# More room for weight combinations, later loads and single-pass degrees at the beginning of a graph and attention kernel

## The chip, the core and the metric

The kernel runs on one core of a Trainium2 chip. The metric is the device time of one execution in microseconds (us). Five engines work side by side, each in the order of its own instructions: TensorE (PE in the profile; its weight loads are PEld), VectorE (DVE), ScalarE (ACT), GpSimd (POOL) and SyncE (SP), which here only issues transfers. They wait for each other by semaphores. [...]

## The reference

32 batches of 512 nodes with 512 features, one adjacency matrix. Each batch passes a graph layer and an attention layer, both with a residual and a LayerNorm:

```python
a = adj.astype(x.dtype); deg = a.sum(axis=1)
mi = einsum('bkd,od->bko', x, Wi); mj = einsum('bkd,od->bko', x, Wj)
x = layernorm(x + deg[None, :, None] * (mi + b) + einsum('ij,bjo->bio', a, mj))
q, k, v = heads(x @ Wq.T + bq), heads(x @ Wk.T + bk), heads(x @ Wv.T + bv)   # 8 heads of 64
scores = where(adj == 0, -inf, q @ k.T / 8)
x = layernorm(x + (softmax(scores) @ v) @ Wo.T + bo)
```

## The kernel before

The kernel multiplies weights by a scheme of seven products of 256 x 256 blocks in place of eight ("pieces" 1 to 7). It needs sums and differences of each weight's quarters. They are made once, at the beginning, stored to DRAM, and later loaded again and again through a ring of seven buffers:

```python
RING = 7
def combine(name, eng, part):
    w = W[name]
    a11, a12, a21, a22 = [w[j][:, :, Q * i:Q * i + Q] for i in range(2) for j in range(2)]
    t = [work([P, 2, N], "e", 4) for _ in range(2 - part)]      # "e": four buffers in all
    t = [u[:, c].rearrange("p (c i) -> p c i", c=2) for u in t for c in range(2)]
    if part == 0:
        s1, s2, s4 = t[:3]
        eng.tensor_tensor(s1, a21, a22, op=OP.add)              # L252
        eng.tensor_tensor(s2, s1, a11, op=OP.subtract)          # L253
        eng.tensor_tensor(s4, a12, s2, op=OP.subtract)          # L254
        ...
    else:
        s3, n22 = t
        eng.tensor_tensor(s3, a11, a21, op=OP.subtract)         # L260
        eng.tensor_scalar(n22, a22, -1.0, 1.0, ...)             # L261
        ...
    for i, u in made:
        WS[name, i] = dram.tile(...)
        nc.sync.dma_start(WS[name, i], u)                       # L265
```

A buffer of a name is given out in turn; whoever takes one again waits until its last readers, here the stores, are done. All loads and stores of this part go through SyncE's queue, in order. The loads at the start, in that order:

```python
load adj, x[0], wi, wj, wv, wq, wk            # 1 MB each
load_x(1)
for q in range(4):
    load_xa(1, q)                             # L113: x[1] in 32 x 32 blocks, pieces of 128 B
wo = load_wo()                                # L166: eight transfers
...                                           # later: b0, bo, bq, bk on GpSimd's queue, bv on SyncE's (L221)
```

`xa` holds x in blocks, so that VectorE can turn it with a transpose of 32 x 32 blocks (L339, `l0_turn`), which GpSimd then multiplies with the degrees. There is one buffer of the name `xa`. The adjacency matrix is turned by TensorE; ScalarE copies it to `adjT` (fp32), VectorE to `adjR` (float32r). The degrees come out of a product with ones:

```python
for jc in range(NC):
    nc.tensor.matmul(pd, ones, adjT[:, jc, :], ...)             # L193, fp32
```

The first batch's graph layer runs with plain products (`plain`, L604), interleaved with the combinations:

```python
def first():
    # half(name, i) is combine(name, engine, i); wi, wj on GpSimd, the others on VectorE
    return [g[0], ..., g[1], g[2], half("wv", 0), g[3], base 0, base 1, half("wv", 1),
            y[0], scaled 0, half("wq", 0), half("wi", 0), y[1], scaled 1, half("wq", 1), half("wi", 1), fold 0,
            y[2], half("wk", 0), half("wj", 0), scaled 2, n[0], y[3], half("wk", 1), half("wj", 1), n[1], fold 1, scaled 3]
# g: gather with adj (L325); y: plain product, residual, LayerNorm statistics (L604, L606, L289, L291)
# scaled: LayerNorm applied by ScalarE (L296); n: turn by TensorE (L353)
```

Then the beginning runs phase c of batch 0 (q, k and v by pieces, L427; the first product of each is copied by ScalarE to p, L434; VectorE adds the others, L456, L465, L472) and phase a of batch 1 (gather, turns, four more pieces of k):

```python
def phase_a(n):
    for i in range(DC):
        res += g[i:i + 1] + k[i:i + 1] + [z(l0_turn, n, i)]
        ...
        if n == 1 and i in (1, 3):
            res += [z(combine, "wo", nc.vector, i // 2)]

PERIODS = [first() + phase_c(0) + phase_a(1)]
```

After it the first scoring period begins: scores (L481), exponential (L485), mask (L486), values (L503), with the pieces of the next batches' graph layers and projections between them. Phase c of later batches also loads the next x:

```python
if i in (6, 7) and 0 < n < B - 1:
    res += [z(load_xa, n + 1, 2 * (i == 7) + (f is v[i]))]
```

Of the kernel before, what the change touches and what calls it, by code (L numbers as in the profile page):

```python
# [10 lines left out]
FR = mybir.dt.float32r  # L11
# [6 lines left out]
P = 128  # L18
# [7 lines left out]
def gnn_attention_kernel(  # L26
# [36 lines left out]
    nc = tc.nc  # L63
    B, N, D = x.shape
    NC = N // P
    DC = D // P
# [13 lines left out]
    def work(shape, name, bufs, dtype=FT):  # L80
        return pools.work.tile(shape, dtype, name=name, bufs=bufs)

    def big():
        return work([P, 4, N], "big", 6)

    def mm_tile(bank):
        return psum.tile([P, 512], FT, name="mm" + bank, bufs=1)
# [7 lines left out]
    def turn_tile():  # L95


        return sc_tile()[:, 0, :]
# [9 lines left out]
    def load_xa(b, q):  # L108

        if q == 0:  # L110
            XA[b] = work([P, DC, N], "xa", 1)
        src = x[b].rearrange("(t p) (c q f) -> q p c t f", p=32, q=4, f=32)
        nc.sync.dma_start(XA[b][32 * q:32 * q + 32].rearrange("p c (t f) -> p c t f", f=32), src[q])  # L113

    def load_x(b):
        XT[b] = work([P, NC, D], "xh", 3)
        nc.sync.dma_start(XT[b], rows(x[b]))
# [12 lines left out]
    def load_w(t, src, eng):  # L130
        eng.dma_start(t, rows(src))
        return t
# [15 lines left out]
    ones = const.tile([P, P], FT, name="ones")  # L148
# [5 lines left out]
    for name, src in (("wv", wvT), ("wq", wqT)):  # L154
        t = load_w(work([P, NC, D], "v", 2), src, nc.sync)
        W[name] = [t[:, 0:2, :], t[:, 2:4, :]]
    load_halves("wk", wkT, "q", nc.sync)
    load_x(1)
    for q in range(4):
        load_xa(1, q)  # L160

    def load_wo():
        t = work([P, NC, D], "xh", 3)
        for h in range(4):
            for g in range(2):
                nc.sync.dma_start(t[32 * h:32 * h + 32, 2 * g:2 * g + 2], woT.rearrange("(g h r d) o -> g h d r o", g=2, h=4, r=2)[g, h])  # L166
        return t

    wo = load_wo()
# [6 lines left out]
    def turned(adj_f, t, also=None):  # L176
        for jc in range(NC):
            pt = turn_tile()
            for ic in range(NC):
                nc.tensor.transpose(pt[:, ic * P:(ic + 1) * P], adj_f[:, ic, jc * P:(jc + 1) * P], ident)  # L180
            nc.scalar.copy(t[:, jc, :], pt)
            if also is not None:
                nc.vector.tensor_copy(also[:, jc, :], pt)
        return t
# [3 lines left out]
    adjR = const.tile([P, NC, N], FR, name="adjR")  # L188
    adjT = turned(adj_f, big(), adjR)
    deg_r = const.tile([P, N], FT, name="deg_r")  # L190
    pd = mm_tile("a")
    for jc in range(NC):
        nc.tensor.matmul(pd, ones, adjT[:, jc, :], start=(jc == 0), stop=(jc == NC - 1))  # L193
    deg_c = const.tile([P, NC], FT, name="deg_c")

    SPLIT = {}
# [44 lines left out]
    def ring_tile():  # L241
        return work([P, 2, Q], "ring", RING)

    def combine(name, eng, part):

        w = W[name]
        a11, a12, a21, a22 = [w[j][:, :, Q * i:Q * i + Q] for i in range(2) for j in range(2)]
        t = [work([P, 2, N], "e", 4) for _ in range(2 - part)]
        t = [u[:, c].rearrange("p (c i) -> p c i", c=2) for u in t for c in range(2)]
        if part == 0:  # L250
            s1, s2, s4 = t[:3]
# [3 lines that stand above are left out]
            made = ((6, s2), (5, s1), (3, s4))  # L255
            if name == "wo":
                made += ((1, a11), (2, a12))
        else:
            s3, n22 = t
            eng.tensor_tensor(s3, a11, a21, op=OP.subtract)  # L260
            eng.tensor_scalar(n22, a22, -1.0, 1.0, op0=OP.mult, op1=OP.mult)  # L261
            made = ((7, s3), (4, n22))
        for i, u in made:
            WS[name, i] = dram.tile([P, 2, Q], FT, name=f"{name}_{i}")
            nc.sync.dma_start(WS[name, i], u)  # L265
# [115 lines left out]
    def quarter(src, j, n):  # L381
        return src[:, 2 * j:2 * j + 2, Q * n:Q * n + Q]
# [168 lines left out]
    def z(f, *a):  # L551
        return (0.0, f, *a)
# [9 lines left out]
    def banks(n):  # L562

        return ("a", "b") if n % 2 == 0 else ("b", "a")

    def phase_a(n):

        A, K = banks(n)
        if n == B:
            return [pc("k", n - 1, i, bank) for i, bank in ((6, K), (5, A), (7, K), (3, A), (4, K))]  # L570
        xq, aq = lambda j, m: quarter(XD[n], j, m), lambda j, m: quarter(AX_T[n], j, m)
        g = [(GA, l0_gather, n, dc, A) for dc in range(DC)]
        k = [pc("k", n - 1, i, K) for i in LATE]
        res = []
        for i in range(DC):
            res += g[i:i + 1] + k[i:i + 1] + [z(l0_turn, n, i)]
            if i in (1, 2):
                res += [z(base, n, i - 1)]
            if n == 1 and i in (1, 3):
                res += [z(combine, "wo", nc.vector, i // 2)]  # L580
            if i == 1:
                res += [z(combos, TX, n, xq, (1,)), z(combos, TA, n, aq, (1,))]
        return res + [z(combos, TX, n, xq, (2,)), z(combos, TA, n, aq, (2,)),
                      z(combos, TX, n, xq, (3, 4)), z(combos, TA, n, aq, (3, 4)),
                      pc("l0", n, 1, A), k[4]]
# [36 lines left out]
    def phase_b(n):  # L622

        m = n - 2
        if m < 0:
            res = []
            side = [z(add_bo, 0, i) for i in range(2)]
            A, K = banks(n)
            for i, bank in ((2, A), (6, K), (5, A), (7, K), (4, K), (3, A)):
                res.append(pc("l0", n, i, bank))  # L630
                if i == 4:
                    res += [z(stats, n, 0)]
                res += side[:1]
                side = side[1:]
            return res + [z(apply, n, 0), z(stats, n, 1), (TR, l0_norm, n, 0), (TR, l0_norm, n, 1)]
        A = banks(n)[0]
        l0 = {i: pc("l0", n, i, A) for i in ORDER}
        return [l0[2], *project(m, 1), l0[6], *project(m, 2), l0[7], z(add_bo, n - 1, 0), *project(m, 6), l0[4], z(stats, n, 0),
                *project(m, 7), z(apply, n, 0), z(h_store, n, 0), l0[5], z(h_load, n, 0), z(add_bo, n - 1, 1), *project(m, 4),
                l0[3], z(stats, n, 1), z(h_turn, n, 0), *project(m, 5)]  # L640

    def phase_c(n):

        m = n - 2
        norm = [(TR, l0_norm, n, ic) for ic in range(NC)]
        h = lambda j, i: quarter(HT[n], j, i)
        A, K = banks(n)
        v, q, k = [{i: pc(kind, n, i, bank) for i in ORDER} for kind, bank in (("v", A), ("q", K), ("k", A))]
        if m < 0:
            res = [v[1]] + ([z(apply, n, 1)] if n else []) + [q[1], v[2], norm[2], norm[3], z(combos, TH, n, h, (1, 2)), k[1],  # L650
                                                             z(combos, TH, n, h, (3, 4)), q[2], k[2]]
        else:
            res = [z(apply, n, 1), z(h_store, n, 1), v[1], *project(m, 3), z(h_load, n, 1), z(stats, m, 0), v[2], z(stats, m, 1),
                   q[1], k[1], z(apply, m, 0), z(h_turn, n, 1), q[2], z(apply, m, 1), z(store, m),
                   z(combos, TH, n, h, (1, 2)), z(combos, TH, n, h, (3, 4)), k[2]]
        side = []
        if n == 0:

            side = [z(graph_forms, 2), None, z(graph_forms, 0), None, z(graph_forms, 1)]
        for i in LATE:  # L660
            for f in q[i], v[i]:
                res += [f] + [g for g in side[:1] if g]
                side = side[1:]
                if i in (6, 7) and 0 < n < B - 1:
                    res += [z(load_xa, n + 1, 2 * (i == 7) + (f is v[i]))]
            if i == 3 and 0 < n < B - 1:
                res += [z(load_x, n + 1)]
            if i == 7 and n + 1 < B:
                res += [z(ahead, n + 1)]
        return res  # L670
# [145 lines left out]
    with tc.If(flag > 0), tc.tile_pool(name="general", bufs=1) as pools.work:  # L816
        wi, wj, wv, wq, wk, wo = [load_w(work([P, DC, D], f"w{i}", 1), src, nc.sync)
                                  for i, src in enumerate((wiT, wjT, wvT, wqT, wkT, woT))]
# [2 lines left out]
        adj_f = big()  # L821
        nc.vector.tensor_copy(adj_f, adj_i)
        adj_t = turned(adj_f, work([P, NC, N], "adj_t", 1))

        bias_m = work([P, NC, N], "bias_m", 1)
        nc.vector.tensor_scalar(bias_m, adj_i, 0.0, -BIG, op0=OP.is_equal, op1=OP.mult)
# [16 lines left out]
        with tc.For_i(0, B, 1) as b:  # L843
# [22 lines left out]
            for hp in range(HP):  # L866
# [6 lines left out]
                for qb in range(NC):  # L873
# [23 lines left out]
                    for kc in range(NC):  # L897
                        for s in range(2):
                            c0 = hp * P + s * HD
                            nc.tensor.matmul(pm[s * HD:(s + 1) * HD, :P], V[g][:, kc, c0:c0 + HD], pT[:, s, kc, :],  # L900
                                             start=(kc == 0), stop=(kc == NC - 1))
# [48 lines left out]
```

## Time and profile before

| what | value |
|---|---|
| time, median of 3 | 3706.04 us (3705.42 to 3707.18) |
| span of the profiled execution | 3701.0 us |
| mean granted TensorE clock | 0.998 |
| moved by DMA | 530.02 MB, mean 143 GB/s |

An entry such as `PE mma L427` names the engine, the tile written and the line of the kernel. `x8` is a count of instructions. A bracket such as `[3.07 <-ACT p L434]` is the idle time of the engine just ahead, and what ended it. SPq is SyncE's queue; the time beside it is the time to issue, not to land. A table by stage gives for each stretch the busy time of PE, PEld, DVE, ACT and POOL with their counts, then TensorE's granted clock, the share of the DMA engines and GB/s.

### The profile page before, as it was taken

What the parts mean: (1) busy time and instruction counts of PE and PEld (TensorE: products, weight loads), DVE (VectorE), ACT (ScalarE), POOL (GpSimd) and SP (SyncE); (2) the same over time, 40 slices, a digit from 0 to 9 for tenths busy, and PEclk for the clock granted to TensorE, in tenths of its full rate; (3) what the DMA queues carried; (4) which work ended last, traced back from release to release, by engine and by line L of the source; (5) the groups of instructions that cost most, each with busy time, mean ns of one, the idle gap of its engine ahead of it and who ended that gap; (6) DMA issues with size and microseconds to landing.
All of it is one profiled execution on the core that took longest, in us unless ns stands there. A gap on an engine that the chain in (4) does not pass through costs nothing.

```text
span 3701.0 us, 49651 instructions
## 1 busy us (share of the span) xinstructions
PE 3664.3 (99%) x18474; PEld 2511.5 (68%) x18474; DVE 2390.7 (65%) x3134; ACT 1028.4 (28%) x1482; POOL 1938.8 (52%) x1985
## 2 busy tenths in 40 slices
PE   8999999999999999999999999999999999999998
PEld 5666666666676767676767666666666676767663
DVE  4566766666666666666666666666666666666665
ACT  2222232322322222222232222232222322222322
POOL 3465545555455564455554555545555545555443
PEclk9999999999999999999999999999999999999999
DMA  7444555455564445554555544555544556445541
GB/s 250 127 126 134 151 151 162 122 143 137 154 159 142 128 135 151 157 155 125 137 143 157 159 135 134 137 149 160 148 132 132 147 151 164 124 136 140 151 137 47
DMA packets 797173, 530.02 MB, mean 143 GB/s; under 512 B 530432, under 2 KB 611840, under 8 KB 796928
## 3 DMA queue, kind: packets, MB, share of 16 engines
q1 hardware_dynamic: 780384, 494.78, 49.7%
q10 hardware_dynamic: 16320, 31.46, 2.3%
q8 instruction: 151, 2.47, 0.3%
q14 instruction: 94, 0.77, 0.1%
q0 software_dynamic: 224, 0.53, 0.0%
HBM read 453.25 MB, written 73.40 MB: 142 GB/s over the span
## 4 chain that ended last, share of the span: by engine, by line
PE 96%; DVE 1%; SPq 1%; POOL 1%; DMA 0%; issue 0%; ACT 0%; POOLq 0%; DVEq 0%; ACTq 0%
PE mma L427 31%; PE mmb L427 31%; PE sc L481 13%; PE ov L503 13%; PE mmb L325 3%; PE mma L325 3%; PE sc L513 2%; SPq L113 0%; DVE rl L522 0%; DVE e L486 0%; DMA wv<-e 0%; SPq L144 0%; DVE st L289 0%; PE sc L727 0%; POOL es L492 0%
## 5 line engine op out<-in xcount | busy, mean ns | idle before, releaser
L485 ACT ACTIVATE sc<-sc 128x1024 f32<-128x1024 f32 x512 | 493.2, 1007 | 1552.5 <-PE sc L481 1546.2
L486 DVE TENSOR_TENSOR e<-sc,edge 128x1024 f32<-128x1024 f32 x512 | 602.2, 1217 | 206.3 <-ACT sc L485 174.3
L427 PE MATMUL mmb<-ring,big 128*128 128x256 f32 x3144 | 731.7, 381 | 0.0
L427 PE MATMUL mma<-ring,big 128*128 128x256 f32 x3112 | 725.3, 382 | 4.2 <-ACT p L434 3.1
L427 PEld LDWEIGHTS mmb<-ring,big 128*128 128x128 f32 x3144 | 592.0, 190 | 131.5 <-issue 26.8
L427 PEld LDWEIGHTS mma<-ring,big 128*128 128x128 f32 x3112 | 586.3, 190 | 135.2 <-issue 26.0
L396 POOL TENSOR_TENSOR big<-big 128x512 f32<-128x512 f32 x376 | 492.7, 1338 | 32.4 <-ACT big L354 11.7
L481 PE MATMUL sc<-q,k 64*128 64x512 f32 x2048 | 509.1, 615 | 0.0
L503 PE MATMUL ov<-e,v 128*32 128x512 f32 x4096 | 492.5, 598 | 4.9 <-DVE oT L538 4.9
L492 POOL TENSOR_TENSOR es<-e 128x1024 f32<-128x1024 f32 x128 | 300.0, 2355 | 351.7 <-DVE e L486 351.7
L427 PE MATMUL mma<-big,ring 128*128 128x256 f32 x1808 | 430.3, 381 | 3.2 <-DVE k L465 3.2
L427 PE MATMUL mmb<-big,ring 128*128 128x256 f32 x1776 | 422.8, 381 | 1.0 <-DVE v L456 1.0
L291 POOL TENSOR_SCALAR mv<-mv 128x1 f32<-128x1 f32 x256 | 49.6, 194 | 671.6 <-DVE mv L290 659.1
L427 PEld LDWEIGHTS mma<-big,ring 128*128 128x128 f32 x1808 | 340.5, 190 | 76.5 <-issue 26.0
L427 PEld LDWEIGHTS mmb<-big,ring 128*128 128x128 f32 x1776 | 334.4, 190 | 73.4 <-issue 26.0
L503 PEld LDWEIGHTS ov<-e,v 128*32 128x32 f32 x4096 | 107.0, 109 | 352.2 <-issue 320.8
L204 POOL TENSOR_TENSOR xlo<-xh,xhi 128x512 fp32r<-128x512 f32 x128 | 163.6, 1289 | 337.6 <-ACT xhi L203 337.6
L481 PEld LDWEIGHTS sc<-q,k 64*128 64x128 f32 x2048 | 176.1, 186 | 207.3 <-issue 205.1
L340 POOL TENSOR_TENSOR big<-big,deg_r 128x512 f32<-128x512 f32 x124 | 173.6, 1400 | 266.3 <-DVE big L339 266.3
L494 DVE TENSOR_TENSOR es<-es,e 128x1024 f32<-128x1024 f32 x250 | 304.2, 1217 | 0.0
L445 DVE TENSOR_TENSOR xh<-xh,mma 128x512 f32<-128x512 f32 x186 | 126.6, 681 | 267.0 <-PE mma L427 267.0
L445 DVE TENSOR_TENSOR xh<-xh,mmb 128x512 f32<-128x512 f32 x186 | 126.7, 681 | 263.0 <-PE mmb L427 263.0
(155 smaller groups left out, 3656.2 us busy)
## 6 DMA issues: line engine op xcount, KB each, us to landing
ring<-wo SPq DMA_DIRECT2D x217, 256.0 KB, 2.8
ring<-wq SPq DMA_DIRECT2D x160, 256.0 KB, 3.9
ring<-wv SPq DMA_DIRECT2D x160, 256.0 KB, 3.4
ring<-wk SPq DMA_DIRECT2D x160, 256.0 KB, 3.2
ring<-wi SPq DMA_DIRECT2D x155, 256.0 KB, 2.7
ring<-wj SPq DMA_DIRECT2D x155, 256.0 KB, 2.7
xh<-in_x_dram SPq DMA_DIRECT2D x32, 1024.0 KB, 5.4
xa<-in_x_dram SPq DMA_DIRECT2D x124, 256.0 KB, 4.0
```

The lines of the kernel that those rows point to most:

```text
L204: nc.gpsimd.tensor_sub(lo, xs, hi.bitcast(FT))
L325: nc.tensor.matmul(pm, parts[w][:, jc, :], adjR[:, jc, :], start=(w == 0 and jc == 0), stop=(w == 1 and jc == NC - 1))
L340: nc.gpsimd.tensor_tensor(XD[b][:, dc, :], XD[b][:, dc, :], deg_r, op=OP.mult)
L396: nc.gpsimd.tensor_tensor(dst, p, q, op=OP.subtract)
L427: nc.tensor.matmul(pm[:, c * Q:(c + 1) * Q], lhs, rhs, start=first, stop=(kc == 1 and n == len(terms) - 1), skip_group_check=True)
L445: nc.vector.tensor_tensor(d, d, pm, op=OP.add)
L481: nc.tensor.matmul(ps[:, s, :], KT[b, hp // 2][r, hp % 2, kc * P:(kc + 1) * P], QT[b, hp // 2][r, hp % 2, :], start=True, stop=True)
L485: nc.scalar.activation(ps, ps, AF.Exp, scale=QSCALE)
L486: nc.vector.tensor_tensor(e, ps, edge[:, kc:kc + 1, :].to_broadcast([P, 2, N]), op=OP.mult)
L492: nc.gpsimd.tensor_add(ES[i], E[i, 0], E[i, 1])
L494: nc.vector.tensor_add(ES[i], ES[i], E[i, kc])
L503: nc.tensor.matmul(PV[g][r][32 * h:32 * h + 32, :], V[b][:, kc, c0:c0 + 32], E[h // 2, kc][:, h % 2, :], start=(kc == 0), stop=(kc == NC - 1))
```

## The change

It does four things. The combinations of wq and of wi's second part get buffers of names that are not yet in use at that time (`xa`, `es`), so that the four `e` buffers are needed less often. wo's combinations move out of phase a of batch 1 into the first scoring period, into `oT` buffers. The second batch's x in blocks is loaded in phase c of batch 0, as for later batches, and no longer ahead of wo. The degrees are computed with float32r operands from `adjR` and a copy of the ones. A branch for unusual inputs, which does not run here, computes its degrees in fp32 as before.

```diff
     load_x(1)
-    for q in range(4):
-        load_xa(1, q)
@@
     deg_r = const.tile([P, N], FT, name="deg_r")
+    onesR = work([P, P], "rl", 1, FR)
+    nc.scalar.copy(onesR, ones)
     pd = mm_tile("a")
     for jc in range(NC):
-        nc.tensor.matmul(pd, ones, adjT[:, jc, :], start=(jc == 0), stop=(jc == NC - 1))
+        nc.tensor.matmul(pd, onesR, adjR[:, jc, :], start=(jc == 0), stop=(jc == NC - 1))
@@
+    def room(name, part):
+
+        if name == "wq" and part == 0:
+            t = work([P, DC, N], "xa", 1)
+            return [t[:, 0:2, :], t[:, 2:4, :]]
+        if (name, part) in (("wq", 1), ("wi", 1)):
+            return [work([P, 2, N], "es", 2)]
+        return [work([P, 2, N], "oT" if name == "wo" else "e", 3 if name == "wo" else 4) for _ in range(2 - part)]
+
     def combine(name, eng, part):
@@
-        t = [work([P, 2, N], "e", 4) for _ in range(2 - part)]
+        t = room(name, part)
@@
-            s3, n22 = t
+            s3, n22 = t[:2]
@@ phase_a
-            if n == 1 and i in (1, 3):
-                res += [z(combine, "wo", nc.vector, i // 2)]
@@ phase_b, the layer-0 pieces of batch 1, in the first scoring period
                 if i == 4:
                     res += [z(stats, n, 0)]
+                if i in (2, 6):
+                    res += [z(combine, "wo", nc.vector, int(i == 6))]
@@ phase_c
-                if i in (6, 7) and 0 < n < B - 1:
+                if i in (6, 7) and n < B - 1:
                     res += [z(load_xa, n + 1, 2 * (i == 7) + (f is v[i]))]
@@ the branch for unusual inputs
+        pd = mm_tile("a")
+        for jc in range(NC):
+            nc.tensor.matmul(pd, ones, adj_t[:, jc, :], start=(jc == 0), stop=(jc == NC - 1))
+        nc.scalar.copy(deg_r, pd)
```

## The prediction

> **What bounds the kernel now.** I read the page first: the span, the busy shares and the 40 slices.
>
> ```profile
> span 3701.0 us, 49651 instructions
> PE 3664.3 (99%) x18474; PEld 2511.5 (68%) x18474; DVE 2390.7 (65%) x3134; ACT 1028.4 (28%) x1482; POOL 1938.8 (52%) x1985
> ...
> PE   8999999999999999999999999999999999999998
> ```
>
> TensorE is busy in 3664.3 of 3701.0 us, so 36.7 us of idle time are left in the whole execution. Only the first and the last slice are below 9. The change touches only the beginning, so the next view is the table of busy time by stage.
>
> ```profile
> 8.00:16.00 8.00, 7.45 (x26) 4.60 (x25) 2.76 (x4) 3.82 (x7) 3.26 (x4) 1.00 1.04 391
> 52.00:72.00 20.00, 15.38 (x56) 10.32 (x55) 9.59 (x18) 6.11 (x10) 13.07 (x18) 0.91 0.79 279
> 104.00:112.00 8.00, 4.83 (x23) 3.80 (x22) 7.93 (x8) 0.58 (x1) 5.35 (x4) 1.00 0.36 130
> 160.00:300.00 140.00, 140.00 (x717) 96.45 (x718) 90.89 (x118) 40.65 (x61) 73.52 (x69) 1.00 0.52 141
> ```
>
> The first number after the stage's length is TensorE's busy time. From 160 us on it is full: 140.00 of 140.00. Idle time sits in 52 to 72 us (4.62 us, and the granted clock falls to 0.91) and in 104 to 112 us (3.17 us). Who causes it is told by the waits of TensorE between 20 and 160 us:
>
> ```profile
> PE mma L427 <- DVE k L465: 3.2, 1, 3.2
> PE mma L427 <- ACT p L434: 3.1, 1, 3.1
> PE sc L353 <- ACT xh L296: 1.5, 1, 1.5
> ```
>
> These are three single waits, 7.8 us together; nothing else there exceeds 0.8 us. The timeline gives the cause of each. Columns are start, duration, engine and line; the bracket is the idle time before it.
>
> ```profile
> 11.29 4.23 PE L193 MATMUL mma<-big,ones 128*128 128x512 f32 x8
> 15.08 16.27 SPq L113 DMA_DIRECT2D xa<-in_x_dram  x4
> 31.39 4.63 SPq L166 DMA_DIRECT2D xh<-in_woT_dram  x8
> 39.90 1.33 SPq L265 DMA_DIRECT2D wv<-e  x3
> 43.04 0.69 DVE L254 TENSOR_TENSOR e<-v,e 128x512 f32<-128x512 f32 x1 [7.01 <-DMA wv<-e]
> 51.56 1.26 POOL L254 TENSOR_TENSOR e<-k,e 128x512 f32<-128x512 f32 x1 [5.28 <-DMA wv<-e]
> 52.80 0.69 DVE L260 TENSOR_TENSOR e<-v 128x512 f32<-128x512 f32 x1 [7.53 <-DMA wq<-e]
> 66.27 2.94 PE L427 MATMUL mma<-ring,big 128*128 128x256 f32 x8 [3.07 <-ACT p L434]
> 104.88 1.78 DVE L252 TENSOR_TENSOR e<-xh 128x512 f32<-128x512 f32 x1
> 106.69 1.63 DVE L253 TENSOR_TENSOR e<-e,xh 128x512 f32<-128x512 f32 x1
> 109.70 1.99 PE L427 MATMUL mma<-big,ring 128*128 128x256 f32 x8 [3.17 <-DVE k L465]
> ```
>
> The chain behind the first two waits: the SyncE queue spends 16.27 us issuing the blocked loads of the second batch's x. Behind them, in order, stand wo's load and the bias, so wv's first combinations are stored only at 39.90 us. Four e buffers hold all combinations, so VectorE waits 7.01 and 7.53 us and GpSimd 5.28 us for stores. LayerNorm statistics and scales stand behind these combinations in the same engines' order. The scale of row block 3 (L296) ends at 65.7 us, and only then does ScalarE copy the product p1 for which the matmuls at 66.27 us wait. The third wait is different: wo's first combinations (L252 to L254) occupy VectorE from 104.88 to 109.05 us, and k's addition L465 stands behind them.
>
> [...] the degrees' four fp32 matmuls are eight records spaced 0.43 us, 0.86 us each, against 1.18 us for four float32r matmuls of the same width in L325, about 0.25 us from start to start. [...] L252 and L253 take 1.78 and 1.63 us here where the same form takes 0.69 us at 57 to 59 us. [...] the eight matmuls after the 3.07 us wait take 2.94 us, not 1.89, while those after 1.55 us lose nothing. [...] The blocked loads move 128 B pieces (32 fp32). [...] 16.27 us for four when they follow 8 MB of other loads, but 0.59 us median to issue and 4.0 us to land later.
>
> **The change part by part.**
>
> Degrees. Before: PE goes from the last transpose at 11.29 us to the next one (L318) at 15.36 us, 4.07 us. After: the matmuls need adjR (VectorE casts, the last 12.16 + 0.69 = 12.85 us) and the copied ones (ScalarE, after its last adjT copy at 12.12 us; an estimate of 0.25 us from 0.58 us for four times the width). Three of four passes run before 12.9 us, the last ends near 13.15, and L318 starts near 13.3 us. Gain 15.36 - 13.3 = 2.05 us. All that follows (casts, xlo, gathers) shifts with it: the second split is ready near 18.3 us and needed near 20.3 us.
>
> More room and no early blocked loads. wo is issued from 15.1 us and the bias ends before 30 us, so wv's stores leave by then. wq's parts go to xa and es, wi's second part to es; e is asked for again only by wi (about 33.5 us) and later, each time some 8 us or more after the stores it waits for. In PE's order with L604's spacing of 3.43 us for eight and PE at 24.0 us: the four plain row blocks take 8 x 3.43 = 27.5 us plus one turn of 0.44, to 51.9; the second turn 0.44 and fold 3.44, to 55.8; v1 and q1 to 59.2; v2 to 60.9 us. Is anything late? Row block 3's product ends at 51.9; addition, statistics, three GpSimd steps and the scale (0.7 + 0.9 + 1.3 + 0.8) end near 55.6 us, with GpSimd's combinations of wj's first part (3 x 1.27) done by 51.4. p1's copy after v1 (57.5 us) ends near 58.2, before 59.2. So both waits vanish. In the trace before, the same point (the turn at L353) stands at 69.00 us. Gain so far 69.0 - 60.95 = 8.05 us, of which 2.05 are the degrees' and 6.0 this part's: 1.55 + 3.07 idle, 1.0 slow clock, and the restart after each wait.
>
> wo's combinations moved. They go behind the additions of two layer-0 pieces in the first scoring period. In the gather stage VectorE loses 4.17 us of work and the matmuls at 109.70 would start where the gather ends, near 106.4 us: gain 3.3 us. In their new place VectorE works little (6.48 of 20 us in the stage 120 to 140). With GpSimd running beside them the two parts last about 5 and 3 us. They delay the addition of l0's piece 6 from 126.0 to about 128.2 us, needed at 133.1 by the next piece in its bank. No wait follows by this count.
>
> Second batch's x loaded late. Four loads between the last ring loads of the first phase c. In the times of before, the last is issued near 91 to 93 us; 4 us to land gives 95 to 97, and L339 first needs it at 98.54 us. It fits, by 1.5 us. VectorE idles 1.91 us before the next k addition, so about 3 us of lateness would be absorbed.
>
> Sum: 8.05 + 3.3 = 11.35 us. I subtract 0.8 us for small new waits (the xa risk below at one in five times 2 us, and 0.4 us for contention in the first scoring period). 3706.0 - 10.5 = 3695.5 us. Since PE is full from 160 us on and the number of matmuls there is unchanged, a shift of the start arrives whole at the end.
>
> **Rivals.** First, a transfer takes the place of the stall: the four blocked loads now share the queue with ring loads at 1.73 us per piece. If xa lands 5 us late, L339 blocks VectorE and the k additions: 2 to 4 us back, 3698 to 3700 us. For it: 16.27 us when they were issued early. Against it: later periods issue the same mix, ring loads between, and L339 waits for no such load there. Second, the store waits stay, merely moved: SyncE still works in order and one ring load of wq's combination sits between the stores (4.2 us of wait before). Then only degrees and wo's move pay: 5.4 us, 3700.7 us. Against it: that wait now begins some 10 us earlier. Third, wo's combinations hurt the first scoring period, [...] 1 to 3 us, 3697 to 3699 us. Fourth, the gain is taken back by a later bound; the full stage from 160 us speaks against it.
>
> **Range and chances.** All parts working and no new wait gives 3694.7; one rival gives 3697 to 3701; a further hidden wait removed might give 3692. Range 3692 to 3701 us. All idle time of the beginning together is some 17 us, 0.5%, so more than 2% faster is nearly impossible; 2% slower would need 74 us of new waits in a stage that is full. Chances: faster 0.01, within 2% 0.98, slower 0.01.
>
> **What would show it right or wrong.** Right: degrees as four records near 1 us; no wait of VectorE or GpSimd for stores from e between 20 and 60 us; no ScalarE wait before v2 and a granted clock of 1.00 there; TensorE's wait for L465's addition gone; first scores near 105.5 us instead of 116.81. Wrong: an idle VectorE before the first stream transpose that ends with xa's DMA, a SyncE queue still blocked before wv's stores, or new waits of TensorE for the layer-0 additions between 105 and 150 us.

## The result and the profile after

The changed kernel takes 3694.78 us (median; 3692.91 to 3696.82) against 3706.16 us (3703.53 to 3709.51) before: 11.4 us less, a ratio of 0.9969 with a 95% interval of 0.9956 to 0.9982. That is well inside 2%, and the interval does not touch 1. The predicted 3695.5 us and its range hold.

The page of the changed kernel, in the same three lines as before:

```profile
span 3693.0 us, 49640 instructions
PE 3662.9 (99%) x18470; PEld 2510.3 (68%) x18470; DVE 2393.1 (65%) x3134; ACT 1028.6 (28%) x1483; POOL 1940.0 (53%) x1985
...
PE   9999999999999999999999999999999999999998
```

TensorE's busy time hardly changed (3662.9 against 3664.3 us). Idle time went, and the first slice now shows 9. The table by stage, same stretches as before:

```profile
8.00:16.00 8.00, 6.58 (x24) 4.92 (x23) 3.88 (x6) 3.81 (x8) 3.59 (x4) 1.00 1.05 391
52.00:72.00 20.00, 20.00 (x89) 15.55 (x88) 4.58 (x9) 7.42 (x14) 14.18 (x14) 1.00 0.79 272
104.00:112.00 8.00, 8.00 (x37) 5.79 (x36) 3.23 (x4) 2.51 (x3) 7.92 (x7) 1.00 0.33 98
160.00:300.00 140.00, 140.00 (x722) 94.55 (x719) 93.07 (x121) 39.38 (x56) 69.61 (x66) 1.00 0.55 148
```

From 52 to 72 and from 104 to 112 us TensorE is now full, at a granted clock of 1.00. Of its waits between 8 and 160 us, these are the one that is new and the one that grew:

```profile
PE mma L193 <- ACT rl L190: 0.9, 1, 0.9
PE mma L436 <- DVE v L465: 0.7, 2, 0.5
```

The waits of 3.2, 3.1 and 1.5 us are gone. L193 now waits 0.9 us for the copied ones (L190), and v's additions (L465) cost 0.7 us where they cost 0.3. The timeline of the changed kernel (start, duration, engine and line, idle time before) gives the marks:

```profile
11.85 2.07 PE L193 MATMUL mma<-adjR,rl 128*128 128x512 f32 x4 [0.87 <-ACT rl L190]
14.21 15.11 SPq L164 DMA_DIRECT2D xh<-in_woT_dram  x8
29.48 5.09 SPq L221 DMA_DIRECT2D bv_c<-in_bv_dram  x8
34.69 1.32 SPq L274 DMA_DIRECT2D wv<-e  x3
71.41 2.00 DVE L235 TENSOR_SCALAR edge<-big 128x2048 bf16<-128x2048 f32 x1
86.26 0.59 SPq L113 DMA_DIRECT2D xa<-in_x_dram  x1
91.56 0.70 DVE L348 STREAM_TRANSPOSE big<-xa 128x512 f32<-128x512 f32 x1
106.38 1.99 PE L490 MATMUL sc<-q,k 64*128 64x512 f32 x8
```

Two things here contradict the prediction's working. The four degree products take 2.07 us, not 1. And wo's load now occupies SyncE's queue for 15.11 us, nearly as long as the four blocked loads did, so wv's stores leave at 34.69 us. SyncE's longest wait at that load is for an earlier one, the second batch's x:

```profile
SPq L164 <- DMA xh<-in_x_dram: 4.0, 1, 4.0
```

GpSimd and VectorE also still wait for stores, 2.3 and 1.7 us, though TensorE loses nothing by it.

Single times of one kernel scatter by 2 to 8 us, the longer ones at a lower mean granted clock: 38 executions of the kernel before run from 3701.32 us at 0.999 to 3708.82 us at 0.996. So single parts of some 1 us are read from marks in the traces, one for each kernel. I cut the beginning in three: up to the first plain product, from there to the turn of row blocks 2 and 3 (eight transposes at once), and from there to the first scores.

| kernel | time us (range) | first plain product | to the turn | to the first scores | first scores at |
|---|---|---|---|---|---|
| before | 3706.16 (3703.53 to 3709.51) | 26.03 | 42.97 | 47.81 | 116.81 |
| after | 3694.78 (3692.91 to 3696.82) | 25.13 | 36.95 | 44.30 | 106.38 |
| e buffers alone | 3693.48 (3690.43 to 3695.32) | 25.43 | 38.77 | 43.64 | 107.84 |
| late xa alone | 3698.45 (3695.60 to 3701.65) | 25.77 | 36.96 | 50.09 | 112.82 |
| early xa again | 3698.15 (3696.71 to 3700.06) | 26.58 | 41.55 | 44.30 | 112.43 |
| wo in phase a again | 3698.59 (3696.07 to 3700.47) | 24.41 | 36.96 | 49.44 | 110.81 |
| fp32 degrees again | 3693.49 (3693.18 to 3695.27) | 26.06 | 36.96 | 44.29 | 107.31 |
| extra early products | 3692.88 (3690.31 to 3693.72) | 23.40 | 38.25 | 44.30 | 105.95 |
| the same, early ones | 3691.95 (3690.29 to 3693.54) | 22.89 | 36.95 | 44.30 | 104.14 |
| xa two pieces later | 3695.51 (3694.97 to 3698.01) | 25.02 | 36.96 | 45.95 | 107.93 |
| e alone, wo loaded after | 3692.57 (3690.88 to 3695.12) | 25.69 | 36.95 | 43.65 | 106.29 |
| e alone, ring load last | 3693.44 (3691.97 to 3694.64) | 25.43 | 36.95 | 43.65 | 106.03 |
| all together | 3690.42 (3688.86 to 3692.22) | 23.35 | 36.96 | 42.94 | 103.25 |

Each ratio below is to executions of the kernel before in the same set of runs. Its median was 3706.16 us beside the changed kernel, 3705.46 in the next four rows, 3704.93 in the four after them and 3704.14 in the last three, so times of different sets are up to 2 us apart for that reason alone.

The first mark also moves with the arrival of the adjacency matrix: the second group of transposes starts at 8.43 to 10.25 us, in kernels whose beginning is the same.

### The profile page after: what moved, and what is told of

It reads as the page before. It is cut to its first block, busy times and chain, and to the rows that moved or that the text cites. A ratio compares the mean times of both kernels' runs of the same rounds, so it can differ in the third digit from the quotient of the medians.

```text
span 3693.0 us, 49640 instructions
## 1 busy us (share of the span) xinstructions
PE 3662.9 (99%) x18470; PEld 2510.3 (68%) x18470; DVE 2393.1 (65%) x3134; ACT 1028.6 (28%) x1483; POOL 1940.0 (53%) x1985
## 4 chain that ended last, share of the span: by engine, by line
PE 97%; DVE 1%; POOL 0%; DMA 0%; ACT 0%; SPq 0%; issue 0%; DVEq 0%; ACTq 0%; POOLq 0%
PE mma L436 31%; PE mmb L436 31%; PE sc L490 13%; PE ov L512 12%; PE mmb L334 4%; PE mma L334 3%; PE sc L522 2%; PE mmb L611 0%; PE mma L611 0%; DVE e L495 0%; DVE rl L531 0%; DMA xa<-hd 0%; SPq L376 0%; PE sc L736 0%; DVE st L298 0%
```

## The experiments

### Room taken away, and one part alone

All combinations in e again:

```diff
-        if name == "wq" and part == 0: ...          # xa
-        if (name, part) in (("wq", 1), ("wi", 1)): ... # es
```

> The changed kernel with all combinations of the first five weights in the four e buffers again; late load of xa, wo's move and single-pass degrees stay. Mark to compare: the start of the first scores, 106.38 us in the changed kernel, 116.81 before. Theory (buffers matter of themselves, because wo's and the bias' loads still keep wv's stores back until about 35 us): waits for stores from e return, 2 to 4 us of TensorE idle before 70 us, first scores at 108.5 to 111 us, time 3697 to 3699. Rival (the blocked loads in the queue were the whole cause): first scores within 1 us of 106.4, time near 3695.

Measured: 3693.48 us, ratio to before 0.9965 (0.9953 to 0.9978), first scores at 107.84 us. In this trace the waits for stores are back, as the timeline of this kernel shows:

```profile
36.27 1.32 SPq L269 DMA_DIRECT2D wv<-e  x3
47.74 1.27 POOL L258 TENSOR_TENSOR e<-k,e 128x512 f32<-128x512 f32 x1 [5.09 <-DMA wv<-e]
49.01 0.69 DVE L264 TENSOR_TENSOR e<-v 128x512 f32<-128x512 f32 x1 [7.38 <-DMA wq<-e]
62.37 1.99 PE L431 MATMUL mma<-ring,big 128*128 128x256 f32 x8 [1.54 <-ACT p L438]
```

VectorE and GpSimd wait as before, but of these two waits, 12.5 us together, only 1.54 us reach TensorE. The stretch grows by 1.8 us, just below the 2 to 4 expected. Neither forecast holds: first scores come 1.46 us later, between the rival's 1 us and the theory's 2.1 us, and the time is not above the changed kernel's.

The next stretch is 0.65 us shorter than in the changed kernel, since TensorE waits 0.3 us for v's additions, not 0.7. It is 0.3 us in all five kernels with e alone, the kernel before among them. VectorE's pass L235 takes 1.22 us in the kernel before and 2.00 us in the changed kernel. So the room itself costs 0.65 us here. Why the pass is slower is not shown.

The kernel before with the late load alone:

```diff
-    for q in range(4):
-        load_xa(1, q)
-                if i in (6, 7) and 0 < n < B - 1:
+                if i in (6, 7) and n < B - 1:
```

> The kernel before with one part alone: the second batch's x in blocks loaded in phase c of batch 0. Combinations all in e, wo's in phase a, degrees fp32. Theory (half of the 6.0 us belongs to the queue, half to the buffers): wv's stores leave near 35 us in place of 39.9, first scores at 112.5 to 114.5 us, time about 3702 to 3704. Rival (the queue is the whole cause): first scores near 110.8, time near 3700.

Measured: ratio 0.9981 (0.9973 to 0.9989), first scores at 112.82 us. wv's stores leave at 34.02 us. The mark is inside my theory's range, but for the wrong reason, and the time of 3698.45 us is below that range. The stretch to the turn is 36.96 us: the late load alone removed the whole 6.0 us there, with only four buffers. What this kernel loses, it loses later, at wo (below).

The blocked loads early again, with es for wq's and wi's second parts:

```diff
+    for q in range(4):
+        load_xa(1, q)
-        if name == "wq" and part == 0: ...          # xa
-                if i in (6, 7) and n < B - 1:
+                if i in (6, 7) and 0 < n < B - 1:
```

> The changed kernel with the blocked loads early again, ahead of wo; as xa is then taken, wq's first part goes back to e, its second and wi's second stay in es. Theory (the queue keeps wv's stores back until about 39 us and with few buffers VectorE waits): first scores 2 to 5 us later than 106.4, time 3697 to 3700. Rival (two more buffers are enough, whatever the queue does): first scores within 1 us of 106.4.

Measured: ratio 0.9981 (0.9973 to 0.9989), stretch 41.55 us, 4.6 us more than after. First scores come 6.05 us later, above the 2 to 5 expected; 1.45 us of that lie ahead of the first plain product. The extra buffers do not make up for stores that leave at 41.05 us.

### wo's combinations back

```diff
+            if n == 1 and i in (1, 3):
+                res += [z(combine, "wo", nc.vector, i // 2)]
-                if i in (2, 6):
-                    res += [z(combine, "wo", nc.vector, int(i == 6))]
```

> The changed kernel with wo's combinations back in phase a of batch 1 (their buffers stay oT). Theory: TensorE waits about 3.2 us for k's addition again, first scores 3.3 to 3.6 us later, near 109.8 us, time near 3698. Rival (with the blocked x landing late the additions stand differently and the wait is halved): 1 to 2 us later, time near 3696.5.

Measured: ratio 0.9978 (0.9969 to 0.9987); the last stretch is 49.44 us, 5.1 us more, where 3.3 to 3.6 were expected. The wait itself is the expected 3.19 us. The rest is in the durations after it:

```profile
102.02 2.82 PE L436 MATMUL mma<-big,ring 128*128 128x256 f32 x8 [3.19 <-DVE k L474]
104.63 4.52 PE L436 MATMUL mmb<-ring,big 128*128 128x256 f32 x16
108.99 1.89 PE L436 MATMUL mma<-big,ring 128*128 128x256 f32 x8
```

Eight matmuls take 2.82 us, not 1.99, and sixteen 4.52, not 3.62, before the pace is 1.89 again. The table by stage of this kernel agrees: the clock (the number after GpSimd's count) is 0.63.

```profile
102.00:106.00 4.00, 3.98 (x12) 3.26 (x13) 4.00 (x5) 0.00 (x0) 1.68 (x1) 0.63 1.01 329
```

In the kernel before, a wait of 3.17 us at this place was followed by a clock of 1.00 (110 to 114 us) and eight matmuls in 1.99 us. The kernel with the late load alone lost still more, 3.78 and 4.86 us for the same two groups. Where the eight matmuls kept to 1.99 us, the wait cost about 3.4 us (47.81 - 43.65, against e alone, less 0.77 us of slow transposes). Where they took longer, it cost 5.1 us here and 6.4 us with the late load alone (50.09 - 43.65). The eleven times of this kernel fall into two groups, five of 3696.07 to 3697.01 us at a mean clock of 0.999 and six of 3698.59 to 3700.47 us at 0.998. That fits a clock that falls in some executions only, but one alone was traced.

In their new place, with GpSimd busy beside them (L451 and L387 in the changed kernel), the two parts took 5.10 and 2.57 us, where about 5 and 3 were estimated. The third operation takes 1.64 us there. In the trace before, where GpSimd's L396 had ended at 107.77 us, the same one (L254, from 108.36 us) took 0.69 us. What slows VectorE there is not shown.

### Degrees, and matmuls at half pace

fp32 degrees again:

```diff
-    onesR = work([P, P], "rl", 1, FR)
-    nc.scalar.copy(onesR, ones)
-        nc.tensor.matmul(pd, onesR, adjR[:, jc, :], ...)
+        nc.tensor.matmul(pd, ones, adjT[:, jc, :], ...)
```

> The changed kernel with the degrees in fp32 from adjT and without the copied ones. Theory (the single passes run at half rate, 0.43 us each, and start 0.9 us later because of the copied ones): worth only 0.3 to 0.9 us; from the last transposes' start (9.01 us) to the first plain product 16.5 us as before, first scores at 106.6 to 107.3 us. Rival (the step of the prediction): 2.05 us, first scores near 108.4 us, time near 3697.

Measured: ratio 0.9971 (0.9959 to 0.9983), first scores at 107.31 us, 0.93 us later. Free of the matrix's arrival, from the second group of transposes to the first plain product: 16.50, 17.44 and 17.35 us in the three kernels with fp32 degrees; 16.12, 16.59, 16.33, 15.92, 16.59, 16.91 and 16.00 us in the seven with float32r degrees and no extra products. The means are 17.10 and 16.35: the degrees are worth about 0.75 us, though the two groups overlap. The fp32 products of this kernel:

```profile
10.48 5.06 PE L191 MATMUL mma<-big,ones 128*128 128x512 f32 x8
```

The first four of these eight records start 0.85 us apart, the last four 0.43 us, and the turn after them takes 0.60 us. So the pace doubled while they ran.

Extra products of the identity while TensorE waits for the adjacency matrix (their results are not used):

```diff
+    def busy(n):
+        t = ov_tile()
+        for _ in range(n):
+            nc.tensor.matmul(t[:, :P], ident, ident, start=True, stop=True)
...
+        busy(6)                     # ahead of the first transpose; 5 more among the first four, 8 after
```

> The changed kernel with some twenty extra fp32 products of the identity with itself (128 columns, results unused) while TensorE waits for the adjacency matrix: six ahead of the first transpose, five within the first four, eight between and after the others. Theory (the array is at half rate until about 15.8 us because it was idle in parts): the four degree products take about 1 us in place of 2.07, the turn after them 0.6 in place of 1.05, first xhi 1.2 in place of 1.57; first scores 1 to 2 us earlier, 104.4 to 105.4 us. Rival (0.43 us is what these first float32r products cost, waits for their operands included): no change or up to 0.5 us later from the extra products.

Measured: ratio 0.9964 (0.9951 to 0.9978). The timeline of this kernel:

```profile
11.66 1.21 PE L204 MATMUL mma<-adjR,rl 128*128 128x512 f32 x4
12.71 0.60 PE L338 MATMUL sc<-ident,xh 128*128 128x128 f32 x4
13.07 1.18 PE L345 MATMUL mmb<-adjR,xhi 128*128 128x512 f32 x4
```

The same four products take 1.21 us, not 2.07, the turn 0.60 and the gather 1.18. In the changed kernel the turn took 1.05 and the gather 1.57 us. From the first degree product to the first plain product it is 11.74 us against 13.28. From start to start the degree products had stood 0.43 us apart in the changed kernel (0.59 us after the first) and stand 0.26 us apart here. So these matmuls had run at little more than half their pace, though the clock column reads 1.00 for 8 to 16 us in the changed kernel, and with TensorE kept at work ahead of them they did not. First scores came only 0.4 us earlier, not the 1 to 2 us expected: this time wv's stores left at 36.19 us, and TensorE waited 1.03 us for p1's copy in spite of the room.

With the copied ones made by ScalarE ahead of the adjacency copies:

```diff
     nc.gpsimd.memset(ones, 1.0)
+    onesR = work([P, P], "rl", 1, FR)
+    nc.scalar.copy(onesR, ones)
```

> As warm, and the copied ones are made by ScalarE ahead of the adjacency copies, so that the degree products wait for nothing but adjR. Theory: TensorE's 0.87 us wait ahead of the degrees vanishes, the first three products start up to 0.8 us earlier, the end is set by the last adjR (12.3 us): 0.2 to 0.6 us better than warm, first scores at 104 to 105 us, time 3692.5 to 3693.5. Rival: no better than warm.

Measured: ratio 0.9966 (0.9953 to 0.9978), first plain product 0.5 us earlier than in the run before it, first scores at 104.14 us. Of the 0.5 us, 0.3 us is the matrix's earlier arrival (second group of transposes at 8.93 us, not 9.25), so the early ones gave about 0.2 us. The extra products had already filled most of the 0.87 us wait. The rest of the gain at the first scores is p1's wait, gone in this run, whose stores of wv left at 33.68 us.

### How late xa may come

```diff
-                if i in (6, 7) and n < B - 1:
+                if n == 0 and i in (7, 4):
+                    res += [z(load_xa, n + 1, 2 * (i == 4) + (f is v[i]))]
+                if i in (6, 7) and 0 < n < B - 1:
```

> The changed kernel with the four blocked loads of the second batch two pieces (3.5 us) later in phase c of batch 0. Theory (they land about 1 us before the first stream transpose at 91.56 us needs them, and VectorE's 1.9 us of idle time after it absorbs some): the first transpose waits 2 to 3 us for xa, TensorE loses 0.5 to 2 us, first scores at 107 to 108.4 us. Rival (the ring's loads set the pace and move too, or the slack is larger): no wait, first scores at 106.4 us.

Measured: ratio 0.9976 (0.9966 to 0.9986). The last of the four loads is issued at 89.65 us, 3.4 us later than in the changed kernel, and VectorE waits 1.83 us for it, as its timeline shows beside TensorE's:

```profile
93.37 0.71 DVE L348 STREAM_TRANSPOSE big<-xa 128x512 f32<-128x512 f32 x1 [1.83 <-DMA xa<-in_x_dram]
96.72 3.45 DVE L354 SCALAR_TENSOR_TENSOR xh<-b_r,deg_c,xh 128x512 f32<-128x512 f32 x2 [1.16 <-POOL xlo L204]
100.09 0.68 DVE L474 TENSOR_TENSOR k<-mma,k 128x512 f32<-128x512 f32 x1
100.83 1.99 PE L436 MATMUL mma<-big,ring 128*128 128x256 f32 x8 [1.38 <-DVE k L474]
```

So the slack was 3.4 - 1.8 = 1.6 us; the prediction had 1.5. Beyond it hardly anything is absorbed: the base additions L354 now start after a wait of 1.16 us for GpSimd and take 3.45 us, not 2.39, and k's addition comes at 100.09 in place of 97.90 us.

### Why the stores were late

Back to e alone, and wo loaded after wv's stores:

```diff
-    wo = load_wo()
...
-half("wv", 1),
+half("wv", 1), z(last_load),        # last_load: the same load of wo
```

> The run with all combinations in the four e buffers again (late xa, wo's move, single-pass degrees kept), and in addition wo's load issued after wv's combinations are stored, not ahead of them. Mark: from the first plain product to the turn before phase c, 36.95 us with no wait, 38.77 in the run with e alone. Theory (what counts is when wv's stores leave the queue): they leave before 30 us, VectorE and GpSimd wait for no store of wv, the stretch is 36.95 us though there are only four buffers. Rival (the queue is also held by the ring's load of a combination of wq, which waits for its own store, about 4 us): still 38 to 39 us.

Measured: ratio 0.9967 (0.9954 to 0.998), the stretch 36.95 us with four buffers. TensorE has no wait in it, though not all of the theory holds: GpSimd still waits 1.4 us for wv's stores, and GpSimd waits 3.2 and VectorE 4.3 us for wq's. The queue of this kernel:

```profile
14.96 13.47 SPq L219 DMA_DIRECT2D bv_c<-in_bv_dram  x8
28.55 1.41 SPq L267 DMA_DIRECT2D wv<-e  x3
34.24 6.46 SPq L164 DMA_DIRECT2D xh<-in_woT_dram  x8
```

Eight bias loads of 0.2 KB each now take 13.47 us to issue, where they took 3.72 us in the kernel before. At this place SyncE of the changed kernel waits for loads ahead of it, 4.0 us for x and 2.3 us for wq: wo's load, which stands next there, is held until they have landed. Here the biases stand next.

Back to e alone, and the seventh ring load after all stores:

```diff
-        if f[1] is combine:
+        if f[1] is combine and (f[2] == "wv" or f[2] == "wj" and f[4] == 1):
             prefetch()
```

> The run with all combinations in the four e buffers again, and in addition the seventh ring load (wq's combination) issued after all stores of combinations, not between them. Theory (the block in the queue is the second half of the wait): GpSimd's wait of 5 us for wv's stores and VectorE's of 7.4 us for wq's shrink by about 4 us each, the stretch from first plain product to the turn is 36.95 us. Rival (wv's late stores alone decide): 38 to 39 us.

Measured: ratio 0.997 (0.9958 to 0.9982), the stretch 36.95 us. The waits did not shrink by 4 us each as expected: GpSimd still waited 5.3 us for wv's stores, VectorE 6.5 us for wq's. In this run wv's stores left at 34.53 us, and the late load alone, with stores at 34.02 us, had no wait of TensorE either. So this run does not tell whether the ring load mattered.

### All together

wo after wv's stores, the ring load last, extra products and early ones, and VectorE's three passes over the adjacency matrix in its idle time before phase c:

```diff
-            side = [z(graph_forms, 2), None, z(graph_forms, 0), None, z(graph_forms, 1)]
+            side = []
-(2 * PC, fold, 1), z(scaled, 3)]
+(2 * PC, fold, 1), z(scaled, 3), z(graph_forms, 2), z(graph_forms, 0), z(graph_forms, 1)]
```

> The changed kernel with the extra early products and early ones of the earlier run, wo's load after wv's stores, the seventh ring load after all stores, and VectorE's three passes over the adjacency matrix (edge, comparison, sum) moved from phase c of batch 0 to the end of the first part, where VectorE idles 12 us. Theory: no wait of TensorE for v's additions (0.7 us less), no waits for stores whatever the transfers do; first scores at 103 to 103.8 us, time 3690.5 to 3692. Rival (the passes, now beside GpSimd's combinations, delay those [...] and the pieces wait for them): first scores not earlier than 104.1.

Measured: 3690.42 us (3688.86 to 3692.22), ratio to before 0.9962 (0.9948 to 0.9975), first scores at 103.25 us, 3.1 us before the changed kernel's. TensorE's wait for v's additions is gone. It is faster than the kernel before. Against the changed kernel the marks speak for it, but the times hardly do: the two intervals overlap, and of the 4.4 us between the medians 2.0 us are the difference of the two sets.

## Why the prediction was right or wrong

The total was right, 10.5 us predicted and 11.4 measured. In part this is luck: the degrees' term was 1.3 us too large, and against that stood the 0.8 us set aside for small waits, 0.2 us more than predicted from wo, and 0.5 us from an adjacency matrix that arrived earlier in the trace after. At the first scores the traces differ by 10.43 us (11.3 predicted, 116.81 - 105.5), and the terms there are:

**Degrees: 2.05 us predicted, about 0.75 measured.** The step that failed is "L318 starts near 13.3 us". It took the 0.25 us spacing of L325, which was measured later in the trace, from 15.71 us on. Here it was 0.43 us; with the extra products it was 0.26. The 0.87 us wait for the copied ones had been counted. Measured from the second group of transposes, which starts 0.52 us earlier here than in the kernel before, the turn starts 0.94 us later than predicted (13.72 + 0.52 = 14.24 us). The turn and the gather after it, slow too (0.71 and 1.40 us to the next start, not 0.35 and 1.02), lose 0.36 and 0.38 us more, so this trace keeps 0.4 us of the 2.05. A sign of the slow start stood in the prediction's own numbers: eight records 0.43 us apart take 3.44 us, and 4.07 us pass from the first to the turn.

**Room and late load: 6.0 us predicted, 6.02 measured (42.97 - 36.95), but the cause was half wrong.** The step that failed is "wo is issued from 15.1 us and the bias ends before 30 us, so wv's stores leave by then". They left at 34.69 us, 5.2 us earlier than before: wo's load now stood behind the same earlier loads and took almost as long to issue as the blocked loads had (15.11 us, not 16.27), so their pieces of 128 B were not what held the queue. The 5.2 us were enough: the late load alone gives the whole 6.0 us. "The restart after each wait" is 0.17 us at each in the trace before: at the pace ahead of them (3.43 us for eight of L604, 1.73 for eight of L427) the matmuls after the two waits would have started 1.72 and 3.24 us earlier, and the waits are recorded as 1.55 and 3.07 us. The room is a reserve for late stores, and it costs 0.65 us at v's additions. In two runs wv's stores left 10.8 us after the first plain product: with room the stretch was 36.95 us, without it 38.77. At 14.5 us, with part of the room, it was 41.55. With the stores at 36.19 us, 12.8 us after, the full room still left a wait of 1.03 us. Each of these figures is from one trace.

**wo's combinations: 3.3 us predicted, 3.51 measured (47.81 - 44.30).** That figure holds 0.8 us of slow transposes at the start of the old stretch (1.81 against 1.04 us for eight), and v's additions take 0.65 us off it; without both, wo's own part is 3.4 us. Put back into the changed kernel the old place costs 5.1 us, with a clock of 0.63 from 102 to 106 us; the prediction had counted on 3.3 us. In the new place no wait came of it, as counted.

**xa late: predicted to fit by 1.5 us; it fits by 1.6.** That "about 3 us of lateness would be absorbed", on the ground that VectorE idles 1.91 us, was wrong: of a wait of 1.83 us for xa, 1.65 us reached TensorE.

**Small new waits: 0.8 us allowed.** v's additions wait 0.4 us more and cost 0.65 us; neither xa nor the first scoring period added one. Of the rivals none came true, though the second named the queue rightly: it stayed blocked, only not for long enough to matter. "A shift of the start arrives whole at the end" held nearly: of the 10.43 us, 9.87 are left near 3600 us. In the two profiled executions the drain then lost another 1.3 us to a clock of 0.72 near 3640 us, where the kernel before kept 1.00, and 0.6 us went after the last matmul, so their spans differ by 8.0 us. The medians differ by 11.4 us, as the profiled execution of the kernel before, 3703.08 us, was 3 us faster than its median.

## What to carry to other kernels

When an engine stalls on buffer reuse, look first at when the release leaves its queue: here an earlier store made four buffers enough, and more buffers bought only tolerance, at a cost of 0.65 us elsewhere. When shortening a product that follows idle stretches, take its duration from a place that follows such stretches too: here products of one form stood 0.43 us apart behind waits of 0.55 and 0.87 us, and 0.26 us apart once TensorE had been kept at work. Before moving work into another period, count that period's waits instruction by instruction: here that gave no new wait for wo's combinations and 1.5 us of slack for xa, and none and 1.6 us were measured. Idle time of an engine is not slack by itself: VectorE's 1.91 us absorbed 0.2.

## What the runs showed of the hardware that was not expected

In these kernels the time to issue depended on the loads ahead in the queue and hardly on the item itself: behind the same 8 MB the next item took 16.27 us (four blocked loads), 15.11 us (wo) or 13.47 us (eight loads of 0.2 KB).

A TensorE wait at the same place was followed by longer matmuls in two kernels (3.19 us, then eight in 2.82 us at a clock of 0.63; 3.18 us, then eight in 3.78 us) and not in a third (3.17 us, then eight in 1.99 us at a clock of 1.00). After the wait of 3.07 us before the change eight took 2.94 us. In the drain a wait of 2.00 us was followed by a clock of 0.72 in the changed kernel, and one of 1.98 us by 1.00 in the kernel before. So the length of a wait alone did not decide it in these traces; what did is not shown.

In the changed kernel the clock column read 1.00 (8 to 16 us) while the degree products stood 0.43 us apart, in place of 0.26 us in the run with extra products.
